# Transposed row maxima written into the unused half of the row sums' PSUM bank, one half step earlier

## The chip, the cores and the metric

The kernel runs on one core of a Trainium2 chip. The time is the device time of one execution in microseconds; the core's engines are named as in the profile: PE (TensorE, matrix multiply), PEld (its weight loads), DVE (VectorE), ACT (ScalarE), POOL (GpSimd) and SP (SyncE, which issues the DMAs).

## The reference

One transformer block on 2048 tokens of width 512, in float32, with attention and feed-forward side by side:

```
xn  = layernorm(x)
out = x + attention(xn, w_qkv, w_o) + ffn(xn, gate, up, down)
attention: 16 heads of 32, causal, softmax(q k^T / sqrt(32)) v, then w_o
ffn:       (gelu_tanh(xn Wg^T) * (xn Wu^T)) Wd^T, 4096 wide, 4-bit weights with block scales
```

The softmax subtracts each row's maximum: with q and k weights eight times the usual size the scores are large, and the maximum can't be left out.

## The kernel before

The heads are taken in pairs p = 0 to 7, the queries in blocks qb of 512 in the order 1, 2, 3, 0 (`ORDER`), the keys in tiles kt of 128. A pair has 40 *steps*: for block qb there are 4*qb full key tiles and then 4 diagonal ones.

A score is computed twice. First with queries on the partitions, for the maxima: `score_rows` (L209) multiplies, `maxima` (L228, L233, on DVE) reduces along the keys. Then with keys on the partitions, for the values: `score_cols` (L280) writes minus the maximum to every key row, `add_scores` (L295) adds the scores, `exponentials` (L309, L315 to L319, on ACT) makes the probabilities.

Between the two, the maxima have to turn from columns to rows. When a block's maxima are complete, `split` (L240) negates them on DVE (L243) and POOL cuts each into three bfloat16 parts (L249, L251), placed in a buffer `parts` of 128 queries x 4 x 128 columns, where a pair uses 64 of the 128 columns. It then notes the work as *due* four steps later. `rows_from_parts` (L255) does it: four transposes on PE (L261) into a PSUM tile `pm`, and one copy on ACT (L264) of the 64 partitions that this pair uses into `neg`, which L280 later reads. `rows_when_due` (L266) is called at the start of every step, does at most one such piece, and counts the steps in `tick`.

There are three stretches of attention. The first (to 185 us) has layernorm, projections and the maxima of pairs 0 and 1. The second, 240 steps for pairs 0 to 5, makes probabilities of pair p and maxima of a pair ahead in the same step. The third does pairs 6 and 7 together. After it come the output projection and the feed-forward.

PSUM has eight banks of 128 partitions x 512 float32: three for `ps_s` (L209, and some projections), three for `ps_t` (L280, and `pm`), and `m0` and `m1` of `ps_m`, one each. A step of the second stretch takes two tiles of `ps_t` and two of `ps_s`. `m0` holds the sums of values `av` (L343) of the current block; `m1` holds its sums of probabilities `rows` (L354), which use partitions 64 to 127 alone. `open_sums` (L362) takes both banks for a new block, just ahead of the block's first value matmul. That is the fourth step of the block: for blocks 1 to 3 the first values (`attend_pair`, L366) are due two steps after the second step, for block 0 (`attend_diagonal`, L380) three steps after the first. In blocks 1 to 3 the first row sums follow a step later; in block 0 they follow the first values at once.

The order is written out by hand: every engine runs its instructions in the order in which the program issues them, and waits between engines are derived from the tiles that they read and write. A step of the second stretch (L579 to L615) issues, in this order:

1. `rows_when_due`: PE transposes, ACT copy, if one is due
2. PE: two L280 into `ps_t`, L209 into `ps_s`, L295 into `ps_t`
3. `run_due`: PE value and row-sum matmuls of earlier steps, `open_sums` with them
4. ACT: the exponentials of this step's `ps_t` tiles; DVE: the maxima of its `ps_s` tiles
5. `keep_attention` for a finished block: ACT copies `av` out of `m0` (L429, or L426), DVE copies `rows` out of `m1` (L430), ACT moves one half (L433), POOL adds (L434)
6. POOL: sums of two probability tiles (L395); in some steps a normalization (L445, L447), or a projection on PE

A finished block's copies are issued in the step just before the next block's `open_sums`.

Of the kernel before, what the change touches and what calls it, by code (L numbers as in the profile page):

```python
# [37 lines left out]
BF16 = mybir.dt.bfloat16  # L38
# [8 lines left out]
P = 128  # L47
# [5 lines left out]
TB = 512  # L53
# [25 lines left out]
def block_kernel(  # L79
# [10 lines left out]
    nc = tc.nc  # L90
# [23 lines left out]
    with (  # L114
# [19 lines left out]
        ident_h = const.tile([P, P], BF16, tag="ident_h", name="ident_h")  # L134
# [57 lines left out]
        tops, negs = {}, {}  # L192
# [42 lines left out]
            if left[p, qb] == 0:  # L235
                split(p, qb)

        due, tick = [], [0]

        def split(p, qb):  # L240

# [13 lines left out]
        def rows_from_parts():  # L255

            _, p, qb, buf = due.pop(0)
            og, half = p // 2, slice(64 * (p % 2), 64 * (p % 2 + 1))
            pt = ps_t.tile([P, TB], BF16, tag="t", name=f"pm{p}_{qb}")
            for i in range(4):  # L260
                nc.tensor.transpose(pt[:, i * P : (i + 1) * P], buf[:, i, :], ident_h)  # L261
            if (og, qb) not in negs:
                negs[og, qb] = negp.tile([P, TB], BF16, tag="neg", name=f"neg{og}_{qb}")
            nc.scalar.copy(negs[og, qb][half], pt[half])  # L264

        def rows_when_due():  # L266
            if due and tick[0] >= due[0][0]:
                rows_from_parts()
            tick[0] += 1

        def score_cols(p, n, pool):

# [61 lines left out]
        avs, rows, sums = {}, {}, {}  # L334
# [27 lines left out]
        def open_sums(p, qb):  # L362
            avs[p, qb] = ps_m.tile([P, TB], F32, tag="m0", name=f"av{p}_{qb}")
            rows[p, qb] = ps_m.tile([P, TB], F32, tag="m1", name=f"rows{p}_{qb}")

        def attend_pair(p, n, prob_a, prob_b, c0, c1):  # L366

            qb, kt = steps[n]
            if kt == 0 and c0 == 0:
                open_sums(p, qb)  # L370
            add_values(p, n, prob_a, 0, kt == 0 and c0 == 0, False, (c0, c1))
            last = kt == 4 * qb - 4 and c1 == TB
            add_values(p, n + 1, prob_b, 1, kt == 0 and c0 == 0, last, (c0, c1))
# [6 lines left out]
        def attend_diagonal(p, n, prob):  # L380
            qb, kt = steps[n]
            if kt == 0:
                open_sums(p, qb)
            last = kt == 4 * qb + 3
            add_values(p, n, prob, 0, kt == 0, last)
            add_rows(p, qb, [prob[:, h] for h in range(2)], kt == 0, last, (kt - 4 * qb) * P)
            if last:
                full.append((p, qb))
# [154 lines left out]
        for b in range(NTB):  # L543
            n = first[b]
            if b + 1 < NTB:
                statistics(b + 1)
                normalize(b + 1, 0)
            project(0, b, 0)
            project(0, b, 1)
            for i in range(4):  # L550
                if b + 1 < NTB:
                    flip(b + 1, i)
                full_width = [value_halves(4 * b + i)] * 2
                if b >= 2:
                    full_width += [project_halves(*later.pop(0))] * 2
                for j in range(b + 1):
                    rows_when_due()
                    tiles = [score_rows(0, n, ps_s), score_rows(1, n, ps_t)]
                    for p in range(2):
                        maxima(p, n, tiles[p])  # L560
                    if j == 0 and i < 3 and b + 1 < NTB:
                        normalize(b + 1, i + 1)
                    n += 1
                    for _ in range(-(-len(full_width) // (b + 1 - j))):
                        next(full_width.pop(0))
# [13 lines left out]
        for m in range((NP - 2) * STEPS):  # L579
            p, n = divmod(m, STEPS)  # L580
            at[0] = m

            ahead = p + 3 if p % 2 == 0 else p + 1
            og, own = p // 2, m % (2 * STEPS)
            rows_when_due()
            ps = score_cols(p, n, ps_t)
            ps_max = score_rows(ahead, n, ps_s)
# [6 lines left out]
            qb, kt = steps[n]  # L594
# [30 lines left out]
            if og + 2 == NOG and own == max(places_own) + 1:  # L625

                wo = []
                for i in range(0, NOG, 2):
                    t = wa.tile([P, 2, H], F32, tag="wqk", name=f"wo{i}")
# [43 lines left out]
            yield  # L673

        pending = []
        early = [(i, k) for i in range(2) for k in range(NK)]
        rest = iter(())
        for s, n in enumerate(together):
            rows_when_due()
            two = [score_cols(NP - 2, n, ps_t), score_cols(NP - 1, n, ps_s)]  # L680
            for i in range(2):
# [5 lines left out]
            qb = steps[n][0]  # L687
# [12 lines left out]
            if early and s % 2 == 0 and not diagonal(together[s + 1]):  # L700
                i, k = early.pop(0)
# [389 lines left out]
```

## Time and profile before

| What | Value |
|---|---|
| median of 3 runs | 1958.79 us (1956.99 to 1959.99) |
| the profiled execution | 1956.68 us, span in the trace 1954.6 us |
| PE busy in the span | 1926.6 us (99%) |
| DVE, ACT, POOL busy | 1330.5 (68%), 1102.1 (56%), 938.0 us (48%) |
| the chain that ended last | PE 93%, ACT 3%, POOL 1%, DVE 1%, issue 1% |
| steps of pairs 0 to 5 | 185.0 to 701.4 us of the span |
| feed-forward and output projection | from 819.5 us on |

How to read the lines: the timeline gives the start in us from the span's start, the time that the row covers, engine, line of the kernel, operation, output tile `<-` input tiles, partitions x elements, and a count where equal instructions were merged. In square brackets stands the idle time of the engine before it and what ended it. The rows of a tile give durations in ns as minimum/median/maximum, then the first and last start. A float32 matmul is two instructions on PE here, so its counts are double. Matmuls on different rows or columns of the array overlap, so the time from one start to the next tells more than a duration.

### The profile page before, as it was taken

What the parts mean: (1) busy time and instruction counts of PE and PEld (TensorE: products, weight loads), DVE (VectorE), ACT (ScalarE), POOL (GpSimd) and SP (SyncE); (2) the same over time, 40 slices, a digit from 0 to 9 for tenths busy, and PEclk for the clock granted to TensorE, in tenths of its full rate; (3) what the DMA queues carried; (4) which work ended last, traced back from release to release, by engine and by line L of the source; (5) the groups of instructions that cost most, each with busy time, mean ns of one, the idle gap of its engine ahead of it and who ended that gap; (6) DMA issues with size and microseconds to landing.
All of it is one profiled execution on the core that took longest, in us unless ns stands there. A gap on an engine that the chain in (4) does not pass through costs nothing.

```text
span 1954.6 us, 32601 instructions
## 1 busy us (share of the span) xinstructions
PE 1926.6 (99%) x11699; PEld 1184.1 (61%) x11699; DVE 1330.5 (68%) x2764; ACT 1102.1 (56%) x2298; POOL 938.0 (48%) x1119
## 2 busy tenths in 40 slices
PE   8999999999999999999999999999999999999998
PEld 4433333333333332348888888888888888888886
DVE  5657666567656764388777777777677777777774
ACT  2112665556556666536666666666666666666664
POOL 1001555455545653256555555645455555555551
PEclk9999999999999999999999999999999999999999
DMA  3000000000000001110000000000000000000002
GB/s 129 1 11 12 1 2 2 1 13 2 2 1 12 2 1 37 51 34 23 20 21 20 21 21 18 24 18 22 19 22 19 20 20 21 21 21 21 18 5 87
DMA packets 55394, 39.89 MB, mean 20 GB/s; under 512 B 14784, under 2 KB 47552, under 8 KB 55232
## 3 DMA queue, kind: packets, MB, share of 16 engines
q1 hardware_dynamic: 55232, 37.81, 6.6%
q8 instruction: 92, 1.51, 0.3%
q14 instruction: 70, 0.57, 0.1%
HBM read 33.55 MB, written 4.19 MB: 19 GB/s over the span
## 4 chain that ended last, share of the span: by engine, by line
PE 93%; ACT 3%; POOL 1%; DVE 1%; issue 1%; DMA 0%; SPq 0%; DVEq 0%; POOLq 0%; ACTq 0%
PE gu L943 24%; PE gu L956 12%; PE pd L1006 12%; PE av L343 10%; PE ps_s L209 8%; PE pd L1018 6%; PE ps_qk L165 6%; PE ps_t L280 4%; PE ps_t L295 3%; PE ps_v L516 3%; PE po L898 3%; ACT prob L309 2%; POOL added L395 1%; DVE tops L233 1%; PE pm L261 0%
## 5 line engine op out<-in xcount | busy, mean ns | idle before, releaser
L943 PE MATMUL gu<-xh,gu 128*128 128x512 f32 x1024 | 403.9, 394 | 0.0
L943 PE MATMUL gu<-lm,gu 128*128 128x512 f32 x1024 | 403.7, 394 | 0.0
L233 DVE TENSOR_REDUCE tops<-ps_s 128x1 f32<-128x512 f32 x384 | 245.2, 685 | 155.8 <-PE ps_s L209 120.0
L1027 DVE SCALAR_TENSOR_TENSOR acc<-pd,acc 128x512 f32<-128x512 f32 x512 | 317.1, 682 | 2.4 <-PE pd L1018 2.4
L988 POOL TENSOR_TENSOR parts<-inter,hi 128x512 fp32r<-128x512 f32 x128 | 171.0, 1336 | 278.3 <-DVE hi L984 269.4
L209 PE MATMUL ps_s<-qk,qk 32*128 32x512 f32 (+3 forms) x1280 | 283.4, 576 | 0.0
L309 ACT ACTIVATE prob<-ps_t 128x512 f32<-128x512 f32 x384 | 205.7, 596 | 137.0 <-PE ps_t L295 110.3
L956 PE MATMUL gu<-lm,gu 128*128 128x512 f32 x1024 | 279.7, 395 | 0.0
L980 DVE SCALAR_TENSOR_TENSOR inter<-gu,gate 128x512 f32<-128x512 f32 x128 | 88.5, 692 | 274.7 <-PE gu L956 272.0
L295 PE MATMUL ps_t<-qk,qk 32*128 32x512 f32 (+3 forms) x1280 | 266.9, 535 | 0.0
L1013 ACT ACTIVATE pd<-pd 128x512 f32<-128x512 f32 x512 | 263.4, 583 | 1.1 <-PE pd L1006 1.1
L343 PE MATMUL av<-prob,v 128*32 128x128 f32 (+3 forms) x1856 | 257.6, 425 | 5.5 <-POOL prob L324 2.7
L1006 PE MATMUL pd<-wd,parts 128*128 128x512 f32 x1024 | 259.6, 396 | 0.0
L950 ACT ACTIVATE gu<-gu 128x512 f32<-128x512 f32 x256 | 148.7, 581 | 187.8 <-PE gu L943 187.8
L395 POOL TENSOR_TENSOR added<-prob,prob 128x512 f32<-128x512 f32 x144 | 179.7, 1269 | 104.0 <-ACT prob L309 103.5
L956 PEld LDWEIGHTS gu<-lm,gu 128*128 128x128 f32 x1024 | 192.0, 188 | 47.1 <-issue 0.2
L943 PEld LDWEIGHTS gu<-lm,gu 128*128 128x128 f32 x1024 | 191.9, 187 | 46.6 <-POOL wd L813 0.2
L1006 PEld LDWEIGHTS pd<-wd,parts 128*128 128x128 f32 x1024 | 192.3, 188 | 45.8
L943 PEld LDWEIGHTS gu<-xh,gu 128*128 128x128 f32 x1024 | 192.0, 188 | 45.7 <-ACT wd L812 0.2
L343 PEld LDWEIGHTS av<-prob,v 128*32 128x32 f32 x1856 | 67.2, 108 | 206.2 <-issue 146.3
L987 ACT CAST parts<-hi 128x512 fp32r<-128x512 f32 x128 | 79.7, 623 | 173.3 <-DVE hi L984 173.3
L228 DVE CUSTOM_DVE_ANT_0 ps_s<-ps_s,mask_qk 128x128 f32<-128x128 f32 (+3 forms) x256 | 120.8, 516 | 79.0 <-PE ps_t L295 47.4
(108 smaller groups left out, 2960.4 us busy)
## 6 DMA issues: line engine op xcount, KB each, us to landing
pk<-packed SPq DMA_DIRECT2D x96, 128.0 KB, 2.2
sc<-scales SPq DMA_DIRECT2D x512, 8.0 KB, 1.6
x<-x SPq DMA_DIRECT2D x16, 256.0 KB, 4.5
acc<-x SPq DMA_DIRECT2D x16, 256.0 KB, 3.0
sc<-scales SPq DMA_DIRECT2D x256, 16.0 KB, 1.7
out<-acc SPq DMA_DIRECT2D x16, 256.0 KB, 2.2
wqk<-w_qk SPq DMA_DIRECT2D x4, 512.0 KB, 3.6
wv<-w_v SPq DMA_DIRECT2D x4, 256.0 KB, 6.1
```

Of the source, the lines that this page charges most:

```text
L209: nc.tensor.matmul(ps[:, :w], lhsT=qT[p // 2, qb][rows, i * P : (i + 1) * P], rhs=kT[p // 2, c][rows, :w], start=True, stop=True,)
L233: nc.vector.tensor_reduce(top, ps[:, :w], AX.X, ALU.max)
L295: nc.tensor.matmul(ps[:, c0:], lhsT=kT[p // 2, kt // 4][rows, (kt % 4) * P : (kt % 4 + 1) * P], rhs=qT[p // 2, qb][rows, c0:], start=False ...
L309: nc.scalar.activation(prob[:, h, :], ps, AF.Exp)
L343: nc.tensor.matmul(avs[p, qb][D * j : D * (j + 1), c0:c1], lhsT=v[kt // 4][:, kt % 4, D * head : D * (head + 1)], rhs=prob[:, h, c0:c1], s ...
L395: nc.gpsimd.tensor_tensor(t, prob_a[:, h], prob_b[:, h], ALU.add)
L943: nc.tensor.matmul(ps, lhsT=parts[:, i, k], rhs=mov, start=(k == 0 and i == 0), stop=(k == NK - 1 and i == 1),)
L956: nc.tensor.matmul(ps, lhsT=gu[g, m, j][:, 2, k], rhs=lm[b, k][1], start=False, stop=(k == NK - 1), skip_group_check=True,)
L988: nc.gpsimd.tensor_tensor(parts[:, 1], inter, high, ALU.subtract)
L1006: nc.tensor.matmul(po, lhsT=parts[:, part, i * P : (i + 1) * P], rhs=w[:, part], start=(part == 0), stop=(part == 1),)
L1013: nc.scalar.activation(po, po, AF.Copy, scale=HIGH_SCALE)
L1027: nc.vector.scalar_tensor_tensor(acc[t], po, SUM_SCALE, acc[t], ALU.mult, ALU.add)
```

## The change

The transposes take only the 64 columns that the pair uses, and so write 64 partitions. Where a block's sums are open, they write partitions 0 to 63 of the bank that holds its row sums, seen as bfloat16, instead of a bank of `ps_t`. `open_sums` remembers the bank that it just took, and then does a due piece at once, ahead of the block's first values in the same step; `rows_when_due` at the start of a step is still there. Before the first `open_sums` and in the third stretch, `ps_t` is used as before.

```diff
-        due, tick = [], [0]
+        due, tick, opened = [], [0], []
...
             og, half = p // 2, slice(64 * (p % 2), 64 * (p % 2 + 1))
-            pt = ps_t.tile([P, TB], BF16, tag="t", name=f"pm{p}_{qb}")
+            if opened:
+
+                pt = opened[0][:64].bitcast(BF16)[:, :TB]
+            else:
+                pt = ps_t.tile([P, TB], BF16, tag="t", name=f"pm{p}_{qb}")[:64]
             for i in range(4):
-                nc.tensor.transpose(pt[:, i * P : (i + 1) * P], buf[:, i, :], ident_h)
+                nc.tensor.transpose(pt[:, i * P : (i + 1) * P], buf[:, i, half], ident_h)
             if (og, qb) not in negs:
                 negs[og, qb] = negp.tile([P, TB], BF16, tag="neg", name=f"neg{og}_{qb}")
-            nc.scalar.copy(negs[og, qb][half], pt[half])
-
-        def rows_when_due():
+            nc.scalar.copy(negs[og, qb][half], pt)
+
+        def rows_when_due(step=1):
             if due and tick[0] >= due[0][0]:
                 rows_from_parts()
-            tick[0] += 1
+            tick[0] += step
...
             rows[p, qb] = ps_m.tile([P, TB], F32, tag="m1", name=f"rows{p}_{qb}")
+            opened[:] = [rows[p, qb]]
+
+            rows_when_due(0)
...
         pending = []
+        opened.clear()
```

A piece noted in step m is due at the start of step m+5. The next block's `open_sums` runs in step m+4, where the counter already stands at m+5. So the piece goes in step m+4, between that step's scores and its values. The one exception is the first `open_sums`, at which two pieces are due: one goes there, the other at the start of the next step, into the same bank.

## The prediction

> **What bounds the kernel now.** I read first the busy time by stage, to see where the edit acts, then the rows of the transposes, then the timeline of each engine around one opening of a block of queries. The attention steps that the edit touches are the second stage, 185.0 to 701.4 us.
>
> ```profile
> core 0: us, PE busy (x) PEld busy (x) DVE busy (x) ACT busy (x) POOL busy (x), PEclk, DMA share, GB/s
> ...
> 185.00:701.40 516.40, 508.21 (x5101) 184.28 (x5100) 338.48 (x800) 316.12 (x803) 287.89 (x459) 1.00 0.02 5
> ```
> PE (TensorE) is busy for 508.21 of 516.40 us at full granted clock, every other engine under two thirds, DMA 2%. So PE's queue sets the time. Whatever holds its head is added to the end, since all later stages stand behind it in the same queue. An engine that is idle on average can still hold PE at one point, and that has to be sought in the timeline.
>
> ```profile
> L261 PE MATMUL pm<-ident_h,parts x128: 219/219/230, 63.7 to 713.4; 128*128 128x128 bf16 x128
> L264 ACT COPY neg<-pm x32: 567/580/587, 64.4 to 713.9; 64x512 bf16<-64x512 bf16 x32
> ```
> These are all instructions on the tile pm: 32 groups of four transposes and one copy of 0.58 us each. 25 of the groups move in time: one for each of the 24 openings in this stage, and a second one of the first opening. The six of the first stage and the last keep their bank and their place; their narrower weights save nothing I can price.
>
> The second opening (block 2 of pair 0), PE:
> ```profile
> 207.95 0.85 PE L343 MATMUL av<-prob,v 128*32 128x384 f32 x8
> 208.74 0.40 PE L261 MATMUL pm<-ident_h,parts 128*128 128x128 bf16 x4
> 209.07 0.68 PE L280 MATMUL ps_t<-neg,ones_h 3*128 3x512 bf16 x2
> 209.38 0.70 PE L209 MATMUL ps_s<-qk,qk 32*128 32x512 f32 x2
> ```
> Four transposes take 0.33 us of PE (208.74 to 209.07). Then the first L280 goes, and the second, with L209 right behind it, only at 209.38: a hole of 0.31. The same opening on ACT (ScalarE) and DVE (VectorE):
> ```profile
> 207.11 0.59 ACT L429 COPY both<-av 128x512 f32<-128x512 f32 x1
> 207.74 0.62 ACT L433 COPY aT<-both 64x512 f32<-64x512 f32 x1
> 208.26 1.06 ACT L309 ACTIVATE prob<-ps_t 128x512 f32<-128x512 f32 x2
> 209.35 0.58 ACT L264 COPY neg<-pm 64x512 bf16<-64x512 bf16 x1
> ```
> ```profile
> 207.32 0.69 DVE L430 COPY sums<-rows 64x512 f32<-64x512 f32 x1
> ```
> The hole ends when the *second* exponential of the opening step ends (208.26+1.06=209.32, plus 0.05). The transposes took the third ps_t bank, so both L280 need banks that the opening step used.
>
> **The change part by part.** *Removed: a turn in ps_t.* With two tiles a step in three banks, the second L280 waits for the first exponential of the step before, not the second. That is worth the hole at most: 0.31 us in blocks 2 and 3 of an even pair, 0.45 in those of an odd pair (L280 285.09, L209 285.54 in the same view of pair 1), 0.17 in block 1 (451.62, 451.79), none in block 0 (both 443.44).
>
> The Trainium skill, "Perfetto Trace Analysis", section "Optimization Strategy", says that a gap which keeps repeating on the engine that should be full can mean too few buffers for the next tile. By it alone the holes are the gain, an estimated 5 us off; the sum below goes by what ACT does instead.
>
> *Moved: four transposes, from after the values to before them.* The 0.33 us stay on PE. The data is ready: POOL's last parts instruction ends over 4 us before each opening. No DMA moves. With half the columns they could take less than 0.33, down to no cost; I keep 0.33, the row of the same operation.
>
> *New wait 1: the bank of the row sums.* The transposes write m1, which DVE must have copied out (L430, the wait that stood before the first row-sum matmul). It ends at 207.32+0.69=208.01; the values went at 207.95. A release takes some 0.14 us to reach a matmul (both ends at 441.97, the values start at 442.11), so transposes start at 208.15, 0.20 late. Behind them on PE stand the values.
>
> *Moved on ACT: the copy L264, ahead of the opening step's exponentials.* Here the sum turns. Its duration stays near 0.58 (for odd pairs it now crosses from the lower to the upper partitions, as L433 does at 0.62: up to 0.04 more). The copy starts 0.43 us after the transposes (443.11 to 443.54 with ACT free), at 208.58. The first exponential follows 0.49 later (two take 1.08, one 0.59), at 209.07, ends at 209.66, and L280/L209 go at 209.71, against 209.38: **+0.33**. The hole is not removed; it now waits for copy and first exponential in place of two exponentials, from a later start. The first L280 would be ready at 208.15+0.33+0.79=209.27, so the PE work between covers only part.
>
> Pair 1 by the same steps: L430 ends at 283.34+0.69=284.03, transposes 284.17, copy 284.60, exponential 285.09 to 285.68, L209 at 285.73 against 285.54: **+0.19**. Block 1: L430 ends at 449.87+0.69=450.56, transposes 450.70, copy 451.13, exponential 451.62 to 452.21, L209 at 452.26 against 451.79: **+0.47**. Later steps are full on PE (1.97 us each), so no slack returns this. DVE's maxima come from scores issued before the transposes and do not move; POOL's additions start up to 1 us later, with some 0.4 us left before their reader.
>
> *New wait 2: only in block 0, where row sums follow the transposes at once.*
> ```profile
> 442.11 0.62 PE L343 MATMUL av<-prob,v 128*32 128x512 f32 x2 [0.70 <-ACT both L429]
> 442.12 0.62 PE L354 MATMUL rows<-prob,ones 128*32 128x512 f32 x2
> ...
> 443.11 0.40 PE L261 MATMUL pm<-ident_h,parts 128*128 128x128 bf16 x4
> 443.44 0.39 PE L280 MATMUL ps_t<-neg,ones_h 3*128 3x512 bf16 x2
> ```
> ```profile
> 441.38 0.59 ACT L429 COPY both<-av 128x512 f32<-128x512 f32 x1
> 442.00 0.62 ACT L433 COPY aT<-both 64x512 f32<-64x512 f32 x1
> 442.52 0.42 ACT L315 ACTIVATE clip<-ps_t 128x128 f32<-128x128 f32 x2
> ```
> L430 ends at 441.92, so the transposes start at 442.06. The copy takes the clip's place at 442.52 and ends at 443.10. If the guard of a tile holds for the whole bank, L354, which writes the other 64 partitions, waits for that copy: it starts at 443.15, its two passes and the change to L280 take the 1.00 of now (442.11 to 443.11), L280 at 444.15 against 443.44: **+0.71**. If the guard goes by partitions, the values start at 442.39, L280 at 443.39: -0.05. No row has two engines on different partitions of one bank, so both ends count for the range. The nearest row is the first one above: PE held 0.70 for an ACT copy out of a whole bank. I take +0.71.
>
> The Trainium skill, "PSUM — Partial Sum Buffer", section "PSUM bank collisions raise a hardware error", asks for a semaphore guard by bank and quadrant of 32 partitions, with guarding by bank as the simple version. Quadrants would make this opening free (the rule speaks for the change), the simple version gives the wait; no run here shows which.
>
> *The first opening (190.5 us)* has two groups: the copy delays the first exponential as above, and the second group falls into the new hole. I set it to 0 (from +0.35 for the delay to -0.3 for the group).
>
> *Sum:* block 1 5 x 0.47 = 2.35; blocks 2 and 3 6 x 0.33 + 6 x 0.19 = 3.12; block 0 6 x 0.71 = 4.26; together +9.7 us. The profiled execution took 1956.68 us (span 1954.6), 2.1 under the median of the three runs, 1958.79. So 1966.4 by the profile and 1968.5 by the median; I say 1968, as a median is compared.
>
> **The rivals.** *Guard by partitions:* 2.35 + 3.12 - 6 x 0.05 = +5.2, 1964. For it: partitions are disjoint and their separation may be tracked. Against: each PSUM tile is one bank here.
> *Faster, by the freed third bank:* if the copy delays the first exponential by less than 0.47 (in pair 0 now 208.26, and 209.38-0.05-0.59=208.74 breaks even), the second L280 goes earlier than now. The full price is 6 x 0.31 + 6 x 0.45 + 5 x 0.17 = 5.4 us, less 17 x 0.20 = 3.4 for wait 1: 1953 to 1957. Against: the copy is written ahead of the exponentials, and I work out 209.07.
> *Nothing to see:* the delays fall into slack that the four-step pattern has behind its diagonal steps, or the transposes do not move: 1957 to 1961. Against: the due step's number is reached just at the opening's call, and the steps behind an opening run without holes.
>
> **How the numbers follow.** Whole-bank guard 0.55, guard by partitions 0.30, nothing 0.08, faster 0.07. The range goes from 1960 (guard by partitions with a smaller delay) to 1973 (whole bank, with releases some 0.15 us slower at each opening). A change of 0.2% is 3.9 us, about what a measurement of this kernel can tell from no change. Slower by more: nearly all of the first case and most of the second, 0.80; same: the rest and the third, 0.14; faster 0.06.
>
> **What would show it.** Right: in the new trace the copy L264 stands ahead of the opening's exponentials, the second L280 of the step behind starts some 1.55 us after the transposes, and in block 0 L354 starts after the copy's end. Wrong: an exponential that starts ahead of the copy, holes at L280 shorter than 0.3, L354 beside L343 in block 0, or a stage that still lasts 516 us. A changed time of the last stage (819.5 us on) would mean a cause I have not named.

## The result, and the profile after

| | median (runs) | profiled execution |
|---|---|---|
| before | 1957.89 us (4) | 1956.68 us |
| after | 1966.51 us (4; 1966.36 to 1969.34) | 1966.36 us |

The ratio is 1.0042, 95% interval 1.0029 to 1.0056: slower by 0.4%, 8.6 us between the medians and 9.7 between the profiled executions. Three of the four executions after lie within 0.2 us, while the four before spread from 1956.66 to 1959.99; the last section takes up that spread.

Where the time came from is read stage by stage, with the bounds set at the same work in both traces: the first *max matmul* (the one that writes minus the maximum: L280 before, L284 after) of the second stretch, the first of the third, and the first matmul of the output projection. After (columns: window, its length, busy time and instructions of each engine):

```profile
core 0: us, PE busy (x) PEld busy (x) DVE busy (x) ACT busy (x) POOL busy (x), PEclk, DMA share, GB/s
0.00:185.67 185.67, 177.62 (x716) 76.48 (x717) 119.47 (x308) 31.98 (x58) 9.83 (x45) 1.00 0.11 37
185.67:711.47 525.80, 515.88 (x5101) 187.09 (x5102) 338.24 (x800) 317.74 (x804) 289.44 (x460) 1.00 0.02 5
711.47:829.45 117.98, 112.56 (x1150) 35.14 (x1148) 45.61 (x126) 77.53 (x170) 37.01 (x87) 1.00 0.05 17
829.45:1964.70 1135.25, 1129.46 (x4740) 888.74 (x4736) 826.33 (x1530) 676.09 (x1267) 602.94 (x528) 1.00 0.09 25
```

The second stretch lasts 525.80 us in place of 516.40: +9.4. The two stages behind it are the same within 0.15, and the first is 0.67 longer (the control below, in which nothing but the transposes' form differs, shows 0.6 there too). DVE's and ACT's busy time in the second stretch hardly changed (338.48 to 338.24, 316.12 to 317.74): no work was added there, so it is waiting. PE's own busy time rose from 508.21 to 515.88 us with the same 5101 instructions, so it can't be read as work: it takes in matmuls that ran side by side before and run one after the other now (block 0, below).

The opening of block 2 of pair 0, the one shown before, on PE and on ACT:

```profile
208.54 0.38 PE L265 MATMUL rows<-ident_h,parts 128*64 128x128 bf16 x4
208.85 0.85 PE L347 MATMUL av<-prob,v 128*32 128x384 f32 x8
209.64 0.38 PE L284 MATMUL ps_t<-neg,ones_h 3*128 3x512 bf16 x1
210.21 0.37 PE L284 MATMUL ps_t<-neg,ones_h 3*128 3x512 bf16 x1 [0.19 <-ACT prob L313]
```
```profile
208.22 0.62 ACT L440 COPY aT<-both 64x512 f32<-64x512 f32 x1
208.96 0.58 ACT L268 COPY neg<-rows 64x512 bf16<-64x512 bf16 x1
209.56 1.09 ACT L313 ACTIVATE prob<-ps_t 128x512 f32<-128x512 f32 x2
```

The transposes now stand ahead of the values, and the copy (L268) ahead of the exponentials. The first max matmul is ready at 209.64. The second waits for the first exponential (209.56 + 0.59 = 210.15, plus 0.06): a hole of 0.57, where before it was 0.31.

An opening of block 0, on PE's weight loads, which carry the waits of the matmuls behind them:

```profile
446.89 0.14 PEld L347 LDWEIGHTS av<-prob,v 128*32 128x32 f32 x4
447.87 0.14 PEld L358 LDWEIGHTS rows<-prob,ones 128*32 128x32 f32 x4 [0.84 <-ACT neg L268]
448.85 0.09 PEld L284 LDWEIGHTS <-ones_h 3*128 3x128 bf16 x2 [0.84 <-issue]
```
```profile
447.24 0.58 ACT L268 COPY neg<-rows 64x512 bf16<-64x512 bf16 x1
```

Before, the first row sums started 0.01 us behind the first values and ran beside them (442.11, 442.12). Now they wait for the copy out of the other half of their bank, which ends at 447.24 + 0.58 = 447.82. So the values take 0.98 alone (446.89 to 447.87), and then the row sums another 0.98 alone.

Step by step (start of a step's first max matmul to the next step's, after minus before), the second stretch changed at the openings and almost nowhere else:

| opening | count | foreseen | measured, us each |
|---|---|---|---|
| block 1 | 5 | +0.47 | +0.50 (odd pairs), +0.38 (even) |
| blocks 2 and 3, even pair | 6 | +0.33 | +0.36 |
| blocks 2 and 3, odd pair | 6 | +0.19 | +0.10 |
| block 0 | 6 | +0.71 | +0.82 |
| the first opening | 1 | 0 | -0.19 |
| the other steps | | 0 | -0.29 in all |

The -0.29 is one step, late in block 3 of pair 5; what shortens it was not looked into.

### The profile page after: what moved, and what is told of

It is laid out like the page before. It is cut to its first block, busy times and chain, and to the rows that moved or that the text cites. A ratio compares the mean times of both kernels' runs of the same rounds, so it can differ in the third digit from the quotient of the medians.

```text
span 1964.7 us, 32587 instructions
## 1 busy us (share of the span) xinstructions
PE 1935.5 (99%) x11699; PEld 1187.5 (60%) x11699; DVE 1329.6 (68%) x2764; ACT 1103.3 (56%) x2298; POOL 939.2 (48%) x1119
## 4 chain that ended last, share of the span: by engine, by line
PE 93%; ACT 3%; DVE 1%; POOL 1%; issue 1%; DMA 0%; SPq 0%; DVEq 0%; POOLq 0%; ACTq 0%
PE gu L951 24%; PE gu L964 12%; PE pd L1014 12%; PE av L347 10%; PE ps_s L209 8%; PE pd L1026 6%; PE ps_qk L165 6%; PE ps_t L284 4%; PE ps_t L299 3%; PE ps_v L523 3%; PE po L906 3%; ACT prob L313 2%; POOL added L402 1%; DVE tops L233 1%; PE rows L358 1%
## 5 line engine op out<-in xcount | busy, mean ns | idle before, releaser
L209 PE MATMUL ps_s<-qk,qk 32*128 32x512 f32 (+3 forms) x1280 | 283.0, 576 | 0.0
```

The lines of the kernel that those rows point to most:

```text
L209: nc.tensor.matmul(ps[:, :w], lhsT=qT[p // 2, qb][rows, i * P : (i + 1) * P], rhs=kT[p // 2, c][rows, :w], start=True, stop=True,)
```

## The experiments

The theory: the place is the loss. Ahead of the exponentials the copy delays them, and with them the second max matmul; in block 0 it also holds the row sums, since waits are kept for the whole bank. The free half of the bank is in itself a gain. The rivals: the bank is the loss (its release, its shared use), or the 64-column form of the transposes is.

**The copy behind the exponentials (e1).** Transposes stay where the change put them; in blocks 1 to 3 only their ACT copy moves.

```diff
-            nc.scalar.copy(negs[og, qb][half], pt)
...
+            if hold:
+                held.append((negs[og, qb][half], pt))
+            else:
+                nc.scalar.copy(negs[og, qb][half], pt)
...
-            rows_when_due(0)
+            rows_when_due(0, qb > 0)
...
             prob = exponentials(p, n, ps)
+            while held:
+                nc.scalar.copy(*held.pop(0))
```

> The changed kernel with one thing altered: in the openings of blocks 1 to 3 the ACT copy (L268) is issued behind the opening step's exponentials instead of ahead of them; block 0 is as in the changed kernel. Theory (the copy ahead of the exponentials holds the second max matmul): in the changed kernel's timeline the first max matmul behind the opening is ready at 209.64 and the second at 210.21; both now go at 209.64, 0.57 earlier in each of 17 openings, 9.7 us in all: about 1957, or 0.999 to 1.001 of before. Rival (the wait for the row sums' bank, or the order of transposes and values on PE, is the cost, and ACT has slack): unchanged, about 1966.

Measured: 1958.6 us, 1.0003 of before (0.9995 to 1.0012). The second stretch lasts 518.17 us, 7.6 less than in the changed kernel. The same opening, PE and then ACT:

```profile
210.26 0.38 PE L267 MATMUL rows<-ident_h,parts 128*64 128x128 bf16 x4
210.57 0.85 PE L352 MATMUL av<-prob,v 128*32 128x384 f32 x8
211.36 0.39 PE L289 MATMUL ps_t<-neg,ones_h 3*128 3x512 bf16 x2
211.37 0.70 PE L209 MATMUL ps_s<-qk,qk 32*128 32x512 f32 x2
```
```profile
210.46 1.06 ACT L318 ACTIVATE prob<-ps_t 128x512 f32<-128x512 f32 x2
211.55 0.58 ACT L604 COPY neg<-rows 64x512 bf16<-64x512 bf16 x1
```

Both max matmuls go at 211.36 and L209 at 211.37: no hole. Against the changed kernel an opening gains 0.55 in the nine places where the hole was 0.57, and 0.43 in the eight (blocks 2 and 3 of odd pairs, block 1 of even pairs) where it was 0.45 and not the 0.57 of the expectation. That is 8.4 us; the first opening and the one step of pair 5, both shorter in the changed kernel, take 0.8 of it back. So the copy's place on ACT is more than the whole loss of blocks 1 to 3. What stays against before in these openings is 0.10 us each, the wait of the transposes for DVE's copy of the row sums. The removed hole is worth more than that, but block 0's +0.82 is worth more still: the second stretch is 1.8 us longer than before. The medians (1958.6 against 1958.5 for the executions of before beside it) do not show that; the fastest executions do (1958.41 against 1956.69).

**Block 0 as before (e2).**

```diff
-            opened[:] = [rows[p, qb]]
-            rows_when_due(0)
+            opened[:] = [rows[p, qb]] if qb else []
+            if qb:
+                rows_when_due(0)
```

> The changed kernel, but block 0's openings do as the kernel before: transposes at the start of the next step, into a ps_t bank. Theory (in block 0 the row sums wait for the copy out of their own bank, and lose their overlap with the values): six openings give back 0.82 us each, 4.9 us: about 1961.6, 1.0017 to 1.0025 of before. Rival (block 0's loss is only moved about, since the same transposes and copy stand on PE and ACT a little later): within 1 us of the changed kernel's 1966.5.

Measured: 1963.02 us, 1.0024 (1.0015 to 1.0033). In the trace each of block 0's openings is back within 0.02 us of before, and the others are as in the changed kernel, but for 2.6 us at the first opening and the step before it (last section). The ratio lies in the band that was expected; the median is 1.4 over the 1961.6, and five of the eleven executions took 1961.3 to 1961.5.

**The bank alone (e3).** The call in `open_sums` goes, so the transposes use the free half, but at the start of the next step.

```diff
             opened[:] = [rows[p, qb]]
-
-            rows_when_due(0)
```

> Only one half of the change: the transposes go into the free half of the row sums' bank, but at the start of the next step as in the kernel before, behind the opening's values and exponentials (the call in open_sums is left out). Theory (the bank is a gain, the early place is the loss): no transposes ahead of the values, the copy behind the exponentials, no third ps_t bank taken, so the second max matmul goes with the first: 6 x 0.31 + 6 x 0.45 + 5 x 0.17 = 5.4 us under before, about 1952.5, 0.9965 to 0.998 of before. Rival (writing and reading a bank whose other half is being summed costs in itself, by waits on the whole bank): the row sums of the next step wait for the copy, 0.3 us or more in each of 25 places, at or above before, 1958 to 1966.

Measured: 1952.91 us, 0.9972 (0.9962 to 0.9983), and in a second set of runs on another chip, under the name e7 (below), 1955.04 us, 0.9979 (0.9970 to 0.9988). Faster than before both times. PE, then ACT:

```profile
208.38 0.85 PE L347 MATMUL av<-prob,v 128*32 128x384 f32 x8
209.16 0.41 PE L265 MATMUL rows<-ident_h,parts 128*64 128x128 bf16 x4
209.51 0.39 PE L284 MATMUL ps_t<-neg,ones_h 3*128 3x512 bf16 x2
209.51 0.70 PE L209 MATMUL ps_s<-qk,qk 32*128 32x512 f32 x2
```
```profile
208.69 1.06 ACT L313 ACTIVATE prob<-ps_t 128x512 f32<-128x512 f32 x2
209.78 0.58 ACT L268 COPY neg<-rows 64x512 bf16<-64x512 bf16 x1
```

The first exponential ends at 208.69 + 0.59 = 209.28, before PE gets to the max matmuls, so both go at once. The step-by-step comparison gives -0.29 (even) and -0.43 (odd) in blocks 2 and 3, -0.15 in block 1, 0.00 in block 0; the holes of before were 0.31, 0.45, 0.17 and none. The second stretch lasts 511.57 us, 4.8 less than before.

**The place alone (e4).** Transposes ahead of the values, always into a `ps_t` bank.

```diff
-            if opened:
+            if False:
                 pt = opened[0][:64].bitcast(BF16)[:, :TB]
```

> Only the other half: the transposes stand ahead of the opening's first values, as in the changed kernel, but write a ps_t bank as in the kernel before. Theory (the place is the loss): the copy delays both exponentials, and the second max matmul waits for the second of them, since the third bank is gone: +0.74 (even pairs) and +0.60 (odd) in blocks 2 and 3, +0.88 in block 1, +0.15 in block 0, where no row sum waits: 13 us over before, about 1971, 1.005 to 1.008. Rival (the row sums' bank is the loss): without it the early place costs little, 1956 to 1961.

Measured: 1961.25 us, 1.0019 (1.0010 to 1.0028). The direction is the theory's, the size was not: a quarter of the 13 us, and just past the end of the rival's band of 1956 to 1961. By the time alone the run would not tell the two apart; the timeline does. PE, then ACT:

```profile
208.62 0.41 PE L265 MATMUL pm<-ident_h,parts 128*64 128x128 bf16 x4
208.96 0.85 PE L347 MATMUL av<-prob,v 128*32 128x384 f32 x8
209.75 0.38 PE L284 MATMUL ps_t<-neg,ones_h 3*128 3x512 bf16 x1
210.32 0.37 PE L284 MATMUL ps_t<-neg,ones_h 3*128 3x512 bf16 x1 [0.19 <-ACT prob L313]
```
```profile
209.07 0.58 ACT L268 COPY neg<-pm 64x512 bf16<-64x512 bf16 x1
209.67 1.09 ACT L313 ACTIVATE prob<-ps_t 128x512 f32<-128x512 f32 x2
```

The expectation had the second max matmul wait for the second exponential. It waits for the first (209.67 + 0.59 = 210.26, plus 0.06). The first goes at 209.75, before either exponential has ended, so of the three banks it has the one of the transposes: that is free again when the copy ends (209.07 + 0.58 = 209.65), ahead of both exponentials, and so the two max matmuls need only one bank that an exponential holds. The hole is the same 0.57 as in the changed kernel. By the step comparison this kernel costs +0.26 (even) and 0.00 (odd) in blocks 2 and 3 and +0.28 and +0.41 in block 1, 0.10 less each than the changed kernel, since here nothing waits for DVE; and in block 0 +0.11 (even) and -0.01 (odd) as against +0.82, since here no row sum waits for a copy. So the second stretch is 520.09 us: place alone +3.7, bank alone -4.8, both +9.4. They do not add up, because the early copy takes away the bank's gain and only the shared bank brings the two new waits.

**The form alone (e5), and block 0's transposes hidden (e6, e7).** The control drops both lines in `open_sums`, so that only the 64 columns are left of the change.

> A control: the transposes take 64 columns and write 64 partitions as in the changed kernel, but in the old place and in a ps_t bank for all of them; the row sums' bank is never used for them. Theory (place and bank waits make the whole difference, the form of the transposes none): 0.9993 to 1.0007 of before, 1958 to 1959. Rival (the 128x64 form costs or saves on PE, some 0.1 us at each of 32 places): 3 us off to either side.

Measured: 1959.69 us, 1.0006 (0.9997 to 1.0015). The second stretch lasts 516.57 us against 516.42, and each of the four transposes keeps its 219 ns. The form is no cause.

The other kernel, e6, is the bank alone for blocks 1 to 3, with block 0's transposes early in `ps_t` and their copy behind the exponentials:

```diff
-            opened[:] = [rows[p, qb]]
-            rows_when_due(0)
+            opened[:] = [rows[p, qb]] if qb else []
+            if qb == 0:
+                rows_when_due(0, True)
```

> The late place with the row sums' bank, as in e3, for blocks 1 to 3; in block 0 the transposes stand ahead of the first values but write a ps_t bank, and their ACT copy is issued behind the opening step's exponentials. Theory: PE waits 0.70 us in each of block 0's openings for the ACT copy out of the values' bank; transposes that need neither that copy nor the row sums' bank fit into this wait, so their 0.33 us go in six openings, 2.0 us less than e3: about 1951, 0.9962 of before. Rival (the wait moves on to the next step's tiles, which need banks that ACT frees later): as e3, 1953, or slower.

Beside it on the same chip, as e7, runs the bank alone once more:

> The same kernel as e3, beside e6 on one chip. The same ratio as there, 0.996 to 0.998 of before; about 2 us above e6 if transposes in block 0 can be hidden, equal to it if not.

Measured: e6 1950.23 us, 0.9956 (0.9943 to 0.9968), the fastest of all; e7 1955.04, as told above. That is 4.8 us apart and not the 2 that were expected of e7; by the traces, 2.0 of it is e6's gain and 2.8 a piece of low clock in e7 (last section). In the timeline of e6:

```profile
439.03 0.41 PE L267 MATMUL pm<-ident_h,parts 128*64 128x128 bf16 x4
439.81 0.62 PE L352 MATMUL av<-prob,v 128*32 128x512 f32 x2 [0.36 <-POOL prob L333]
439.82 0.62 PE L363 MATMUL rows<-prob,ones 128*32 128x512 f32 x2
```

The transposes stand in what was a wait of 0.70 us, of which 0.36 is left (the profile names POOL; ACT's copy of the values' bank ends at 439.07 + 0.59 = 439.66, 0.15 before, as in the other openings). Row sums and values run side by side. Each of the six openings is 0.33 us shorter than before, and the second stretch lasts 509.58 us, 2.0 less than with the bank alone: the 6 x 0.33 that was expected.

## Why the prediction was right

*What bounds it.* PE's queue: the 24 openings add up to +9.7 us, one other step gained 0.29, and the stretch ends 9.4 us later. No later stage gave any of it back.

*The hole that does not go.* The step that decided the sign was the copy's place on ACT. It gave +0.33 for the opening that was worked out from the timeline, and +0.36 came; moving that copy alone took 7.6 us out of the second stretch. The profile also showed the one price that the freed bank would have had if the copy had stood elsewhere: 5.4 us by the holes, 4.8 measured with the bank alone (each hole gave back 0.02 less than its length).

*Wait 1, DVE's copy of the row sums.* Put at 0.20 us an opening, it came to 0.10. The release reached PE faster than the 0.14 that I had taken from an ACT copy: DVE ends at 207.79 + 0.69 = 208.48, and the transposes start at 208.54.

```profile
207.79 0.69 DVE L437 COPY sums<-rows 64x512 f32<-64x512 f32 x1
```

*The copy that changes halves.* In half of the openings another error made up for the 0.10. The prediction saw that the copy now goes from the lower to the upper partitions when the maxima belong to an odd pair, and allowed up to 0.04 us for it in the copy's duration. The duration stayed 0.58, but the next ACT instruction starts 0.60 later behind such a copy (208.96 to 209.56) and 0.48 or 0.49 later behind the others, here in pair 1:

```profile
287.01 0.58 ACT L268 COPY neg<-rows 64x512 bf16<-64x512 bf16 x1
287.50 1.07 ACT L313 ACTIVATE prob<-ps_t 128x512 f32<-128x512 f32 x2
```

All 24 openings divide this way: 0.60 in blocks 2, 3 and 0 of even pairs and in block 1 of odd pairs, where the maxima are an odd pair's, and 0.48 or 0.49 in the rest. So in blocks 1 to 3 the first kind came out 0.03 above the number foreseen (+0.36 for +0.33, +0.50 for +0.47), and the second 0.09 below (+0.10 for +0.19, +0.38 for +0.47). The trace before had the same difference on L433: it goes from the upper to the lower half in even pairs, and the next instruction starts 0.52 later (207.74 to 208.26); in odd pairs it goes from the lower to the upper half, and the next starts 0.64 later:

```profile
283.76 0.62 ACT L433 COPY aT<-both 64x512 f32<-64x512 f32 x1
284.40 1.09 ACT L309 ACTIVATE prob<-ps_t 128x512 f32<-128x512 f32 x2
```

What causes the difference was not tried.

*Wait 2, block 0's row sums.* The trace of before could not show whether the guard goes by bank or by partitions. It goes by bank: the wait on the copy stands in the row's bracket, and in the place alone (e4), where the copy reads another bank, values and row sums run side by side again. (A tile fills its bank here, so a guard by tile would look the same.) The choice, at 0.55 against 0.30, was a judgement; with the other guard the same sum would have given 1964. The Trainium skill, "PSUM — Partial Sum Buffer", section "PSUM bank collisions raise a hardware error", calls guarding by bank the simple version of its rule; this kernel has that version, and its price is 0.82 us at each of six openings. Whether the finer guard would run clean here was not tried. My term was 0.71. It had the two passes of values and row sums together behind the wait, 1.00 in all; in fact the values run during the wait and the row sums alone behind it, 0.98 and 0.98, and the copy ended (447.82) just as the values did (447.87).

*The sum.* +9.7 was set, +9.4 came in the second stretch. Block 0 was 0.7 dearer in all; blocks 1 to 3, a first opening that gained 0.19 where I set 0, and the step that gained 0.29 were 0.9 cheaper. That the total came so near is in part luck, since errors of both signs cancelled. The 1968 that was set down is the sum added to the median of three executions (1958.79); added to the profiled execution it is 1966.4, and 1966.51 was measured.

## What to carry to other kernels

An edit that frees a buffer is not done when the buffer is free: write out, engine by engine, what the moved instructions now stand in front of, because a short copy ahead of the work that the next step waits for can eat more than the buffer gave. Two users of one PSUM bank, even on different partitions, may be kept apart as a whole bank, as they were here, so let the second one write where the first one's reader has already had time to run. When a change joins two edits (a new place and a new buffer), run each alone: here, in the second stretch, one was worth -4.8 us, the other +3.7, and the pair cost 9.4.

## What the runs showed that was not expected

The same kernel twice (e3 and e7, on two chips) has medians 2.1 us apart. The profiled executions differ in one short piece. The bank alone, first run, then second run:

```profile
186.00:190.00 4.00, 2.32 (x19) 0.68 (x12) 1.98 (x4) 3.16 (x6) 0.95 (x5) 1.00 0.39 133
190.60:196.80 6.20, 5.66 (x66) 2.30 (x62) 3.98 (x8) 4.04 (x10) 4.45 (x4) 1.00 0.00 0
```
```profile
186.00:190.00 4.00, 2.35 (x19) 0.68 (x12) 1.94 (x4) 3.16 (x6) 1.01 (x6) 1.00 0.40 133
190.60:196.80 6.20, 5.89 (x34) 1.76 (x30) 2.61 (x5) 2.25 (x5) 3.53 (x4) 0.50 0.00 0
```

In the second, the granted TensorE clock (third column from the right) is 0.50 for just under 7 us (190.6 to 197.4); in the stretch shown 34 matmuls pass in place of 66, and the step comparison puts the cost at 2.8 us. The profiled execution of e2 has the same piece (2.6 us), and those of before and after do not. It comes just behind steps in which PE stood idle for 1.19 and 0.54 us, but the same idle times stand there in the traces without it, so they alone do not decide. The executions divide by their mean granted clock: the bank alone took 1951.8 to 1952.9 us in the five executions of e3 and e7 with a clock of 0.999 or 1.000, and 1954.6 to 1957.0 in the thirteen with 0.997 or 0.998. So a median of this kernel can move by 2 to 3 us with the number of such executions, and changes of that size are told more surely from the steps of two traces than from the medians. What triggers it was not tried.
